# A linear-attention and Hadamard feed-forward block: weight sums moved within attention, stores issued later, staged tokens read earlier, down weights split in two stages

## Chip, cores and metric

The kernel runs on one core of one Trainium2 chip. The metric is the device time of one execution in microseconds (us), given as the median of several executions. The profile is of one further execution.

## The reference, cut to what matters

4096 tokens of width 512, all in float32. Attention is causal linear attention with 16 query heads and 4 key/value heads of width 128; a feed-forward block with Walsh-Hadamard transforms (fwht) follows. Both have a residual and a layer norm without weights.

```
q, k, v = x @ Wq.T, x @ Wk.T, x @ Wv.T        # 16, 4, 4 heads of 128
q, k = rope(q), rope(k);  qf, kf = elu(q) + 1, elu(k) + 1
for each token s:                             # running sums over the tokens
    state += kf[s] outer v[s];  z += kf[s]
    out[s] = (qf[s] @ state) / (qf[s] @ z + 1e-6)
x = layernorm(x + out @ Wo.T)
y = fwht(x * SU_ug) / 64
up, gate = y @ W_up.T * (Ws_up * 64), y @ W_gate.T * (Ws_gate * 64)      # 2048 each
h = fwht(silu(gate) * up * SU_dp) / 64
x = layernorm(x + h @ W_down.T * (Ws_dp * 64))
```

## The kernel before

**Number form.** Each operand of a large product is split into a high part, a rounded copy made by ScalarE, and a low part, the difference, made by VectorE or GpSimd (`hilo`, L88 to L90). A product is three matmuls: high by high, high by low, low by high.

**Order.** All DMAs are issued from SyncE's queue by the helper `dma`, whose call is L58, so all of them have that one line. The program is written as Python loops with generators that are stepped by hand (`step`, `go`). The order on each engine is then decided by the tile framework's planner (`TileContext(..., schedule_with_timeline_sim=True)`), which goes through its own simulated time: program order is a priority, and an instruction whose inputs and buffers are there can go ahead of it. Each engine, SyncE's queue too, then runs its own list strictly in order, and a waiting instruction holds all behind it. A pool has a fixed number of buffers for each tag.

**Stages.** There are four:

1. *Attention* (L127 to L507). 16 blocks of 256 tokens are gone through twice, once for each half of the heads: n = 0 to 31, with four slots in each n for its two key heads and two pairs of 64-token chunks. The weights of one half take 24 of the 28 buffers of the pool `wres` (tag `w`, 2 KB each in a partition). In the first half, `load_x` loads and splits the tokens and stores the parts to `xs_d`; the second half loads those parts. `wcomb(p)` prepares gate and up weights for a later stage: it loads four quarter matrices of `wug` into four `wres` buffers, forms four sums and differences on GpSimd (L394) and stores them to `was_d`. It is called in n = 3 to 10.
2. *Wo stage* (L600 to L755). 32 tiles of 128 tokens. For each, numerators are multiplied by the reciprocal of the denominators (`norm_o`), 48 matmuls form the output projection (`ps_wo`, L722), x is added (L734) and, for each two tiles, `layer_norm` normalises the pair, which is stored to `y_d`. From each of the first 12 pairs `wo_front` makes the transformed tokens for gate and up: transpose, sign, Hadamard matmul, butterflies, and seven combinations (`YKEY`) stored to `yq_d` by `put`. `prep_down` transforms the down weights and stores their seven combinations to `wdop_d`. The tile loop steps each front three times for each tile (`fr`). Transformed tokens of the first quarter are loaded by `yload` into the pool `yop` (16 buffers of 4 KB) and split by `ysplit` from tile 26 on.
3. *Gate and up* (L758 to L890). 32 stages: four quarters f of 1024 tokens by eight pairs p of weight tiles. Each stage has seven products s = 0 to 6 (`SEQ`: a seven-multiplication scheme of Strassen's kind for 2 by 2 blocks), each for gate and for up with six matmuls of 128x512 (L833). Results are combined and passed through SiLU; gate times up on GpSimd (L816) gives the blocks H, of which four more combinations are formed on GpSimd (`hS`, L887). Seven blocks a stage go to `hop_d`. `asplit(n + 1, s)` and `aload(n + 2, s)` prepare the next stages' weights. Fronts of the last four pairs run inside stages 1, 3, 5 and 7, with temporaries in the tag `x4` (`xtile`, 2 buffers), which the token loads of later quarters use too. In the last stage (n = 31), `split_b(s)` splits all seven sets of down weights.
4. *Down* (L893 to L985). 8 units of 512 tokens, each with seven products of 48 matmuls of 128x256 (L951). `h_load` fetches four raw tiles for each product, `h_split` splits them, the residual from `y_d` is added, and `finish` normalises and stores the output.

Raw weights of gate and up are loaded into tag `ar` (10 buffers) of the pool `g1`, which closes with stage 3; raw operands of down into tag `hr` (8 buffers) of the pool `d1`, which opens with stage 4 on the same memory.

Of the kernel before, what the change touches and what calls it, by code (L numbers as in the profile page):

```python
# [43 lines left out]
def kernel(  # L44
# [95 lines left out]
    with ExitStack() as es:  # L140
# [296 lines left out]
        for i, (n, g, p) in enumerate(slots):  # L437
# [62 lines left out]
            if sl == (1, 0) and 3 <= n < 11:  # L500
                wcomb(n - 3)
# [41 lines left out]
    def front(i, y2, spool, ptr, phd, alloc):  # L543
        f, c = divmod(i, 4)
        d = alloc[1]([128, 2, 4, 128], F32, "fd")
        for e in range(2):
            ps = ptr([128, 4, 128], "ps_tr")
            for k in range(4):
                T.transpose(ps[:, k], y2[e][:, k * 128:(k + 1) * 128], idt)
            for k in range(4):  # L550
                S.activation(ps[:, k], ps[:, k], AF.Copy, scale=sut[:, k:k + 1])
            hl = alloc[0]([128, 2, 4, 128], F32R, "fhl")
            hilo(hl[:, 0], hl[:, 1], ps)
            yield
# [12 lines left out]
        G.tensor_tensor(q[:, 1], d[:, :, 0:2], d[:, :, 2:4], ALU.subtract)  # L567

        def put(key, x):
            dma(yq_d[f][YKEY.index(key)][:, :, c * 128:(c + 1) * 128], x)  # L570

        put("B11", q[:, 0, 0])
        put("B21", q[:, 1, 0])
        put("B22", q[:, 1, 1])
        put("T3", d[:, 1, 2:4])
        yield
        tt = alloc[1]([128, 3, 2, 128], F32, "ft")
        G.tensor_tensor(tt[:, 0], q[:, 0, 1], q[:, 0, 0], ALU.subtract)
# [43 lines left out]
    with ExitStack() as es:  # L622
# [89 lines left out]
        for t in range(32):  # L712
# [23 lines left out]
            if t % 2:  # L736
                layer_norm(p2, [yp[:, 0], yp[:, 1]], "r1")
                for j in range(2):
                    dma(y_d[t - 1 + j], yp[:, j])
                if t < 24:  # L740
                    fr.append(wo_front(t // 2, [yp[:, 0], yp[:, 1]]))
            if t >= 1:
                step(gd, 4)
            for x in list(fr):
                step(x, 3)
            fr = fr[-2:]
            if 26 <= t:
                for s in ((t - 26,) if t < 31 else (5, 6)):
                    YOPS[s] = ysplit(s, yload(0, s))
# [8 lines left out]
    pgu = ctx.enter_context(tc.tile_pool(name="pgu", bufs=2, space=PSUM, reuse_waits="tile"))  # L758
    BW = [None] * 7

    with ExitStack() as es:
# [5 lines left out]
        def araw(name):  # L767
            return pa.tile([128, 2, 2, 128], F32, tag="ar", name=name, bufs=10)
# [11 lines left out]
        def load_b(s):  # L780
            RAW["b", s] = []
            for j in range(4):
                x = pa.tile([128, 2, 256], F32, tag="ar", name="braw", bufs=10)
                dma(x, wdop_d[s][:, 2 * j:2 * j + 2])
                RAW["b", s].append(x)

        def split_b(s):
            raw = RAW.pop(("b", s))
            ops = [[], []]
            for j in range(2):  # L790
                hl = [wres.tile([128, 2, 256], F32R, tag="w", name=x) for x in ("wdh", "wdl")]
                hilo(*hl, raw[j])
                for l in range(2):
                    ops[l] += [hl[l][:, 0], hl[l][:, 1]]
            hl = [ytile([128, 4, 256], F32R, x) for x in ("wdzh", "wdzl")]
            for j in range(2):
                hilo(hl[0][:, 2 * j:2 * j + 2], hl[1][:, 2 * j:2 * j + 2], raw[2 + j], G if j else V)
            for l in range(2):
                ops[l] += [hl[l][:, r] for r in range(4)]
            BW[s] = ops  # L800

# [3 lines left out]
        yraw = []  # L805
        fr = None
        for n in range(NS):
# [11 lines left out]
            if n in (1, 3, 5, 7):  # L819
                fr = ff_front(12 + n // 2)  # L820
            new = {}
            for s, tag in enumerate(SEQ):
# [3 lines left out]
                for u in (1, 0):  # L826
# [20 lines left out]
                    if s == 5:  # L847
# [30 lines left out]
            def put(key):  # L878
# [3 lines left out]
            for key in ("A11", "A12", "A22"):  # L882
                put(key)
            for key, x0, x1, op in (("S1", "A21", "A22", ALU.add), ("S3", "A11", "A21", ALU.subtract),
# [3 lines left out]
                put(key)  # L888


    with ExitStack() as es:
        pd = es.enter_context(tc.tile_pool(name="d1", bufs=2, reuse_waits="tile"))
        units = [(f, jp) for f in range(4) for jp in range(2)]  # L893
# [4 lines left out]
        HR, HOP, YN, bank = {}, {}, {}, {}  # L898

        def h_load(n, s):  # L900
            f, jp = units[n]
            HR[n, s] = []
            for qd in range(4):
                raw = pd.tile([128, 2, 256], F32, tag="hr", name="hraw", bufs=8)
                dma(raw, hop_d[f][s, jp, :, 2 * qd:2 * qd + 2])
                HR[n, s].append(raw)
            if s == 0:
                YN[n] = []
                for half in range(2):
                    y = (pd.tile([128, 2, 512], F32, tag="yn", name="yres") if half else  # L910
                         xtile([128, 2, 512], F32, "yres"))
                    for j in range(2):
                        dma(y[:, j], y_d[8 * f + 2 * (2 * jp + j) + half])
                    YN[n].append(y)

        def h_split(n, s):
            HOP[n, s] = []
            for qd, raw in enumerate(HR.pop((n, s))):
                hi, lo = (pd.tile([128, 2, 256], F32R, tag="ad", name=x, bufs=20) for x in ("hah", "hal"))
# [11 lines left out]
        h_load(*order[0])  # L931
        h_load(*order[1])
        h_split(*order[0])
        for idx, (n, s) in enumerate(order):
            if idx + 2 < len(order):
                h_load(*order[idx + 2])
            if idx + 1 < len(order):
                h_split(*order[idx + 1])
# [91 lines left out]
```

## Time and profile before

| what | before |
|---|---|
| median of 3 runs (lowest to highest) | 2380.95 us (2379.08 to 2382.65) |
| the profiled execution: its time, its span | 2373.57 us, 2371.9 us |
| mean granted TensorE clock | 0.988 |
| busy: TensorE, VectorE, ScalarE, GpSimd | 2272.3, 1818.6, 1402.0, 1246.1 us |
| DMA traffic, mean rate | 484.16 MB, 204 GB/s |

PE is TensorE, DVE VectorE, ACT ScalarE, POOL GpSimd, and SPq SyncE's queue, which issues the DMAs. Rows name an instruction by its line and by output<-inputs. A busy share is an average over four stages with different limits, so it is to be read by stage: attention lies at about 0 to 970 us, the Wo stage at 970 to 1368, gate and up at 1368 to 2024, and down at 2041 to 2372. The chain of waits is the work that ended last, followed back from the end.

### The profile page before, as it was taken

To read this page: it belongs to the slowest core of one execution; us is meant where nothing else is said; L and a number is where in the kernel's file an instruction comes from. 1 tells how busy PE (TensorE), PEld (TensorE's weight loads), DVE (VectorE), ACT (ScalarE), POOL (GpSimd) and SP (SyncE) were. 2 spreads that over 40 slices of the span, in tenths; PEclk is the share of its full clock that TensorE was granted. 3 is DMA by queue.
4 is the path that set the end of the run, shared out by engine and by line. 5 is a ranking of instruction groups with operands and counts; after the bars stand their busy time and mean duration, and the time that the engine had idled before them with its cause. 6 is when DMAs were issued, how large, how long until landed. Compare 5 with 4: busy or idle time off the path is not lost.

```text
span 2371.9 us, 42234 instructions
## 1 busy us (share of the span) xinstructions
PE 2272.3 (96%) x14432; PEld 2014.1 (85%) x14432; DVE 1818.6 (77%) x2799; ACT 1402.0 (59%) x2482; POOL 1246.1 (53%) x1000
## 2 busy tenths in 40 slices
PE   7999999999999998999999999999999999699998
PEld 6888999989999998788887778778878887699998
DVE  7999998998888889678887776666766767565554
ACT  5666777777777777444443466555655656455553
POOL 3676454454444445377878435555565556533332
PEclk9999999999999999999999999999999999899999
DMA  7676555554444545979897876776765766777673
GB/s 237 212 226 183 168 150 149 157 155 130 132 134 135 141 143 138 304 241 293 272 282 232 283 235 202 243 230 188 225 211 189 240 189 205 235 227 250 222 254 125
DMA packets 369528, 484.16 MB, mean 204 GB/s; under 512 B 68670, under 2 KB 224384, under 8 KB 365344
## 3 DMA queue, kind: packets, MB, share of 16 engines
q1 hardware_dynamic: 369312, 481.45, 65.7%
q8 instruction: 114, 1.87, 0.3%
q14 instruction: 102, 0.84, 0.1%
HBM read 282.76 MB, written 156.76 MB: 185 GB/s over the span
## 4 chain that ended last, share of the span: by engine, by line
PE 78%; DVE 11%; DMA 4%; issue 3%; ACT 3%; POOL 1%; SPq 0%; DVEq 0%; ACTq 0%; POOLq 0%
PE ps_wo L722 15%; PE ps_a L833 13%; PE ps_qk L244 11%; PE ps_da L951 8%; PE ps_b L833 7%; PE ps_num L371 4%; PE ps_db L951 4%; PE ps_c L833 4%; PE ps_s L294 3%; PE ps_v L197 2%; PE ps_dc L951 2%; DVE x L230 1%; DVE sw L234 1%; DVE ps_qk L227 1%; PE ps_sc L337 1%
## 5 line engine op out<-in xcount | busy, mean ns | idle before, releaser
L351 POOL TENSOR_SCALAR_AFFINE_SELECT A<-A 64x512 fp32r<-64x512 f32 x256 | 222.2, 868 | 294.9 <-DVE am L347 197.1
L244 PE MATMUL ps_qk<-xh,wh 128*128 128x256 f32 x1280 | 360.3, 281 | 11.5 <-DVE x L230 7.0
L244 PE MATMUL ps_qk<-xl,wh 128*128 128x256 f32 x1280 | 358.0, 280 | 2.4 <-DVE xl L90 2.4
L244 PE MATMUL ps_qk<-xh,wl 128*128 128x256 f32 x1280 | 357.9, 280 | 0.2 <-DVE wl L90 0.2
L90 DVE TENSOR_TENSOR wol<-A,woh 128x512 fp32r<-128x512 f32 x217 | 228.5, 1059 | 110.9 <-ACT woh L89 91.2
L816 POOL TENSOR_TENSOR cc<-cc 128x512 f32<-128x512 f32 x96 | 146.9, 1532 | 300.7 <-ACT cc L813 153.0
L226 POOL TENSOR_TENSOR sw<-sw,csb 128x512 f32<-128x512 f32 x160 | 220.4, 1379 | 146.1 <-ACT sw L225 136.7
L244 PEld LDWEIGHTS ps_qk<-xh,wh 128*128 128x128 f32 x1280 | 243.3, 190 | 14.0 <-ACT qh L323 3.1
L244 PEld LDWEIGHTS ps_qk<-xl,wh 128*128 128x128 f32 x1280 | 242.6, 190 | 3.7 <-DVE xl L90 2.7
L244 PEld LDWEIGHTS ps_qk<-xh,wl 128*128 128x128 f32 x1280 | 242.6, 190 | 1.5 <-DVE wl L90 0.4
L89 ACT ACTIVATE hah<-hraw 128x512 fp32r<-128x512 f32 x224 | 140.7, 631 | 153.0 <-PE ps_da L951 74.3
L89 ACT ACTIVATE woh<-A 128x512 fp32r<-128x512 f32 x217 | 135.7, 630 | 134.8 <-PE ps_b L833 71.7
L90 POOL TENSOR_TENSOR hal<-hraw,hah 128x512 fp32r<-128x512 f32 x80 | 105.6, 1323 | 207.0 <-ACT hah L89 173.0
L833 PE MATMUL ps_a<-yoh,woh 128*128 128x512 f32 x512 | 202.8, 397 | 3.8 <-ACT sv L840 3.8
L833 PE MATMUL ps_a<-yol,woh 128*128 128x512 f32 x512 | 202.5, 395 | 0.0
L833 PE MATMUL ps_a<-yoh,wol 128*128 128x512 f32 x512 | 199.1, 396 | 0.0
L90 DVE TENSOR_TENSOR hal<-hraw,hah 128x512 fp32r<-128x512 f32 x144 | 103.7, 726 | 123.2 <-ACT hah L89 110.8
L722 PE MATMUL ps_wo<-wh,oh 128*128 128x512 f32 x448 | 179.1, 400 | 11.0 <-DVE yp L734 8.2
L722 PE MATMUL ps_wo<-wh,ol 128*128 128x512 f32 x448 | 178.5, 399 | 0.0
L722 PE MATMUL ps_wo<-wl,oh 128*128 128x512 f32 x448 | 178.2, 398 | 0.0
L840 ACT ACTIVATE sv<-ps_a,wsc 128x512 f32<-128x512 f32 x192 | 127.0, 679 | 43.0 <-PE ps_a L833 42.9
L231 ACT ACTIVATE sw<-x,neg 128x512 f32<-128x512 f32 x160 | 115.3, 721 | 54.5 <-DVE x L230 52.4
(215 smaller groups left out, 7283.1 us busy)
## 6 DMA issues: line engine op xcount, KB each, us to landing
hraw<-hop_d SPq DMA_DIRECT2D x224, 256.0 KB
vd<-vhl SPq DMA_DIRECT2D x128, 256.0 KB
num_d<-num SPq DMA_DIRECT2D x128, 256.0 KB
rb<-rec_d SPq DMA_DIRECT2D x128, 256.0 KB
hop_d<-hS SPq DMA_DIRECT2D x128, 256.0 KB
nt<-num_d SPq DMA_DIRECT2D x31, 1024.0 KB
A<-in_wug_dram SPq DMA_DIRECT2D x93, 256.0 KB
hop_d<-cc SPq DMA_DIRECT2D x64, 256.0 KB
```

The lines of the kernel that those rows point to most:

```text
L89: S.activation(hi, src, AF.Copy)
L90: eng.tensor_tensor(lo, src, hi.bitcast(F32), ALU.subtract)
L226: G.tensor_tensor(sw, sw, sinb, ALU.mult)
L231: S.activation(sw, x1, AF.Exp, bias=neg1)
L244: T.matmul(ps[:, j], W[key][wa][:, k * 128:(k + 1) * 128], B[xa][:, k], start=i == 0, stop=i == 11)
L351: G.affine_select(ah, ah.bitcast(F32), pattern=[[0, 8], [1, 64]], compare_op=ALU.is_ge, fill=0.0, base=0, channel_multiplier=-1)
L371: T.matmul(ps[:, c2], l, r, start=i == 0, stop=i == len(ops) - 1)
L722: T.matmul(ps, l[:, h], r, start=i == 0, stop=i == 47)
L816: G.tensor_tensor(x, x, c.pop(("g", q)), ALU.mult)
L833: T.matmul(ps, w[:, u, k], y[:, k], start=first and i == 0, stop=i == 5, skip_group_check=not first)
L840: S.activation(x, ps, AF.Copy, scale=sc)
L951: T.matmul(ps[:, j], ops[qd][al][:, r, js], BW[s][bl][ip], start=first and i == 0, stop=i >= 45, skip_group_check=True)
```

## The change

- `wcomb` is called in n = 18 to 25, in the second half of attention, instead of n = 3 to 10.
- `front` has two more pauses, one ahead of each group of `put` calls; up to three fronts instead of two are kept in the list.
- A pair of normalised tiles is stored to `y_d` one tile later (the last pair at once).
- Token loads and splits of the first quarter are called at tiles 24 to 30 instead of 26 to 31. Those of a later quarter are called two ahead, the first two of them at the end of stage p = 6.
- Fronts in gate and up start in stages 1, 2, 4, 5; an unfinished one is first stepped to its end.
- The stores of a stage's seven blocks to `hop_d` are called in the next stage, after s = 1, 2, 3, three at a time; the last stage's follow the loop.
- A pool `rp` of 10 raw buffers outlives both stages: it holds raw gate and up weights, raw down weights and raw down operands. In stage n = 31 only three sets of down weights are split, and the first operand of down is loaded; the other four sets are split in the first four steps of the first down unit. The residual's load is called at s = 3 of the unit before. The operand splits of down have 19 buffers instead of 20.

```diff
-            if sl == (1, 0) and 3 <= n < 11:
-                wcomb(n - 3)
+            if sl == (1, 0) and 18 <= n < 26:
+                wcomb(n - 18)
...
+        yield
         put("B11", q[:, 0, 0])
...
+        yield
         put("T1", tt[:, 0])
...
                 layer_norm(p2, [yp[:, 0], yp[:, 1]], "r1")
-                for j in range(2):
-                    dma(y_d[t - 1 + j], yp[:, j])
+                ylast = yp
...
+            if t % 2 == 0 and t or t == 31:
+                for j in range(2):
+                    dma(y_d[t - t % 2 - 2 * (t < 31) + j], ylast[:, j])
...
-            fr = fr[-2:]
-            if 26 <= t:
-                for s in ((t - 26,) if t < 31 else (5, 6)):
-                    YOPS[s] = ysplit(s, yload(0, s))
+            fr = fr[-3:]
+            if 24 <= t < 31:
+                YOPS[t - 24] = ysplit(t - 24, yload(0, t - 24))
...
+    rp = ctx.enter_context(tc.tile_pool(name="rp", bufs=10, reuse_waits="tile"))
...
-            if n in (1, 3, 5, 7):
-                fr = ff_front(12 + n // 2)
+            if n in (1, 2, 4, 5):
+                step(fr, 9)
+                fr = ff_front(12 + (1, 2, 4, 5).index(n))
...
+                if n and s in (1, 2, 3):
+                    for _ in range(3):
+                        if late_puts:
+                            late_puts.pop(0)()
...
-                        if s == 0:
-                            yraw = [yload(f + 1, 0)]
-                        if s < 6:
-                            yraw.append(yload(f + 1, s + 1))
                         new[s] = ysplit(s, yraw[s])
+                        if s < 5:
+                            yraw.append(yload(f + 1, s + 2))
                     else:
                         if s == 0:
                             load_b(0)
                             load_b(1)
-                        split_b(s)
-                        if s + 2 < 7:
-                            load_b(s + 2)
+                        if s in (1, 3, 5):
+                            split_b(s // 2)
+                        if s == 1:
+                            load_b(2)
+                        if s == 5:
+                            h_load(0, 0)
                 step(fr)
+            if p == 6 and f < 3:
+                yraw = [yload(f + 1, 0), yload(f + 1, 1)]
...
-            for key in ("A11", "A12", "A22"):
-                put(key)
+            late_puts = [lambda k=k, put=put: put(k) for k in ("A11", "A12", "A22", "S1", "S3", "S2", "S4")]
...
-                put(key)
+        for put in late_puts:
+            put()
...
-        h_load(*order[0])
+        h_split(*order[0])
         h_load(*order[1])
-        h_split(*order[0])
+        load_b(3)
+        y_load(0)
         for idx, (n, s) in enumerate(order):
-            if idx + 2 < len(order):
-                h_load(*order[idx + 2])
             if idx + 1 < len(order):
                 h_split(*order[idx + 1])
+            if n == 0 and s + 3 < 7:
+                split_b(s + 3)
+            if idx + 2 < len(order):
+                h_load(*order[idx + 2])
+            if n == 0 and s + 4 < 7:
+                load_b(s + 4)
+            if s == 3 and n + 1 < len(units):
+                y_load(n + 1)
```

More of the change, by code (lines that the diff above doesn't have):

```diff
@@ L758, with h_load, load_b, split_b @@
     pgu = ctx.enter_context(tc.tile_pool(name="pgu", bufs=2, space=PSUM, reuse_waits="tile"))
+    rp = ctx.enter_context(tc.tile_pool(name="rp", bufs=10, reuse_waits="tile"))
     BW = [None] * 7
+    HR, HOP, YN, bank = {}, {}, {}, {}
+    units = [(f, jp) for f in range(4) for jp in range(2)]
+    def h_load(n, s):
+        f, jp = units[n]
+        HR[n, s] = []
+        for qd in range(4):
+            raw = rp.tile([128, 2, 256], F32, tag="ar", name="hraw")
+            dma(raw, hop_d[f][s, jp, :, 2 * qd:2 * qd + 2])
+            HR[n, s].append(raw)
+    def load_b(s):
+        RAW["b", s] = []
+        for j in range(4):
+            x = rp.tile([128, 2, 256], F32, tag="ar", name="braw")
+            dma(x, wdop_d[s][:, 2 * j:2 * j + 2])
+            RAW["b", s].append(x)
+    def split_b(s):
+        raw = RAW.pop(("b", s))
+        ops = [[], []]
+        for j in range(2):
+            hl = [wres.tile([128, 2, 256], F32R, tag="w", name=x) for x in ("wdh", "wdl")]
+            hilo(*hl, raw[j])
+            for l in range(2):
+                ops[l] += [hl[l][:, 0], hl[l][:, 1]]
+        hl = [ytile([128, 4, 256], F32R, x) for x in ("wdzh", "wdzl")]
+        for j in range(2):
+            hilo(hl[0][:, 2 * j:2 * j + 2], hl[1][:, 2 * j:2 * j + 2], raw[2 + j], G if j else V)
+        for l in range(2):
+            ops[l] += [hl[l][:, r] for r in range(4)]
+        BW[s] = ops
     with ExitStack() as es:
@@ L767, in araw @@
         def araw(name):
-            return pa.tile([128, 2, 2, 128], F32, tag="ar", name=name, bufs=10)
+            return rp.tile([128, 2, 2, 128], F32, tag="ar", name=name)
         def ff_front(i):
@@ L778, in ff_front @@
                              lambda s, n: pgu.tile(s, F32, tag="a", name=n, bufs=4), (ytile, xtile))
[L780 to L800, printed above, removed]
         for s in range(7):
@@ L804 @@
         NS = 32
-        yraw = []
+        yraw, late_puts = [], []
         fr = None
@@ L870, with put @@
                             load_b(1)
-                        split_b(s)
-                        if s + 2 < 7:
-                            load_b(s + 2)
+                        if s in (1, 3, 5):
[4 more added lines that the diff above has]
+                            h_load(0, 0)
                 step(fr)
+            if p == 6 and f < 3:
+                yraw = [yload(f + 1, 0), yload(f + 1, 1)]
             YOPS.update(new)
             H = {"A11": c["h", 0], "A12": c["h", 2], "A21": c["h", 1], "A22": c["h", 3]}
-            def put(key):
+            def put(key, f=f, p=p, H=H):
                 dma(hop_d[f][WKEY.index(key)].rearrange("j p i t -> p j i t")[:, :, p],
                     H[key].rearrange("p (j t) -> p j t", j=2))
-            for key in ("A11", "A12", "A22"):
-                put(key)
+            late_puts = [lambda k=k, put=put: put(k) for k in ("A11", "A12", "A22", "S1", "S3", "S2", "S4")]
             for key, x0, x1, op in (("S1", "A21", "A22", ALU.add), ("S3", "A11", "A21", ALU.subtract),
@@ L887 @@
                 G.tensor_tensor(H[key], H[x0], H[x1], op)
-                put(key)
+        for put in late_puts:
+            put()
     with ExitStack() as es:
         pd = es.enter_context(tc.tile_pool(name="d1", bufs=2, reuse_waits="tile"))
-        units = [(f, jp) for f in range(4) for jp in range(2)]
         order = [(n, s) for n in range(len(units)) for s in range(7)]
@@ L897, with y_load @@
             order.insert(order.index((n - 1, 5)), (n, 0))
-        HR, HOP, YN, bank = {}, {}, {}, {}
-        def h_load(n, s):
+        def y_load(n):
             f, jp = units[n]
[L902 to L914, printed above, removed]
+            YN[n] = []
+            for half in range(2):
+                y = (pd.tile([128, 2, 512], F32, tag="yn", name="yres") if half else
+                     xtile([128, 2, 512], F32, "yres"))
+                for j in range(2):
+                    dma(y[:, j], y_d[8 * f + 2 * (2 * jp + j) + half])
+                YN[n].append(y)
         def h_split(n, s):
@@ L918, in h_split @@
             for qd, raw in enumerate(HR.pop((n, s))):
-                hi, lo = (pd.tile([128, 2, 256], F32R, tag="ad", name=x, bufs=20) for x in ("hah", "hal"))
+                hi, lo = (pd.tile([128, 2, 256], F32R, tag="ad", name=x, bufs=19) for x in ("hah", "hal"))
                 hilo(hi, lo, raw, G if qd == 1 or (qd == 3 and s % 2) else V)
@@ L929, in finish @@
                 dma(out[t * 128:(t + 1) * 128], y[:, j])
-        h_load(*order[0])
+        h_split(*order[0])
         h_load(*order[1])
-        h_split(*order[0])
+        load_b(3)
+        y_load(0)
         for idx, (n, s) in enumerate(order):
+            if idx + 1 < len(order):
+                h_split(*order[idx + 1])
+            if n == 0 and s + 3 < 7:
+                split_b(s + 3)
             if idx + 2 < len(order):
                 h_load(*order[idx + 2])
-            if idx + 1 < len(order):
-                h_split(*order[idx + 1])
+            if n == 0 and s + 4 < 7:
+                load_b(s + 4)
+            if s == 3 and n + 1 < len(units):
+                y_load(n + 1)
             tag = SEQ[s]
```

## The prediction

> **What bounds the kernel now.** I read the page first, then the busy time of each stage, then the waits of TensorE and the chain of waits at the places where a stage loses time.
>
> ```profile
> PE 2272.3 (96%) x14432; PEld 2014.1 (85%) x14432; DVE 1818.6 (77%) x2799; ACT 1402.0 (59%) x2482; POOL 1246.1 (53%) x1000
> ```
>
> TensorE is busy for 96% of the span: no edit that only unloads another engine gains anything by itself. What can be had is the roughly 100 us in which TensorE idles, or runs thinner than elsewhere. Where that is, the stages show (us, busy time of each engine with instructions in brackets, granted clock, DMA share, GB/s):
>
> ```profile
> 60.00:240.00 180.00, 165.61 (x1283) 153.76 (x1282) 172.24 (x249) 120.39 (x218) 121.25 (x100) 0.98 0.69 210
> 240.00:400.00 160.00, 160.00 (x1312) 152.74 (x1310) 147.89 (x248) 121.81 (x220) 80.75 (x75) 1.00 0.51 147
> 600.00:760.00 160.00, 159.64 (x1297) 151.78 (x1296) 138.94 (x238) 117.56 (x208) 76.65 (x77) 1.00 0.50 139
> 1360.00:1420.00 60.00, 54.79 (x237) 43.09 (x235) 45.54 (x64) 39.67 (x68) 18.42 (x13) 1.00 0.74 245
> 1520.00:1580.00 60.00, 53.19 (x221) 41.27 (x221) 43.62 (x52) 38.13 (x66) 31.70 (x22) 0.97 0.80 255
> 1580.00:1680.00 100.00, 100.00 (x430) 80.53 (x429) 63.77 (x72) 51.79 (x87) 56.78 (x39) 1.00 0.62 194
> 2000.00:2060.00 60.00, 39.82 (x232) 34.30 (x231) 41.96 (x42) 29.75 (x51) 38.11 (x25) 0.86 0.71 234
> 2060.00:2340.00 280.00, 280.00 (x2358) 280.00 (x2357) 161.94 (x330) 145.69 (x240) 90.69 (x70) 1.00 0.72 234
> ```
>
> From 60 to 240 VectorE is full (172.2 of 180) and TensorE waits for it; once that is over, TensorE never pauses. The stages 1580:1680 and 2060:2340 are free of stalls. Holes are at 1360 to 1420, 1520 to 1580, and 2000 to 2060. The same view of the projections alone (L244) gives the first loss exactly: 685 matmuls in 180 us, then 686 in 160, so **20 us** go there.
>
> ```profile
> 60.00:240.00 180.00, 91.43 (x685) 85.22 (x686) 0.98 0.69 210
> 240.00:400.00 160.00, 87.63 (x686) 82.19 (x684) 1.00 0.51 147
> ```
>
> What differs between the two windows is the weight sums (the rows of tile wq: duration min/median/max in ns, first and last start):
>
> ```profile
> L58 SPq DMA_DIRECT2D wq<-in_wug_dram x32: 539/580/1059, 31.5 to 191.8; - x32
> L394 POOL TENSOR_TENSOR wq<-wq x32: 1262/1299/1782, 37.4 to 204.5; 128x512 f32<-128x512 f32 x32
> ```
>
> They stand in the program at blocks 3 to 10 of 28 us each (the chain repeats its projections at 637.41 and 665.35), but were issued from 31.5: the planner pulls work ahead as soon as its buffers are free. Two stalls of the issuing queue (start, duration, instruction), and after them the chain of waits at the last boundary:
>
> ```profile
> 1355.97 2.48 SPq L58 DMA_DIRECT2D yraw<-yq_d  x5
> 1374.18 1.03 SPq L58 DMA_DIRECT2D y_d<-yp  x2
> 1375.32 0.39 SPq L58 DMA_DIRECT2D yraw<-yq_d  x1
> ```
>
> ```profile
> 2022.35 1.44 PE ps_b L833 x5
> ...
> 2033.25 1.27 POOL hS L887
> ...
> 2034.53 0.36 SPq L58
> ...
> 2034.99 5.02 DMA hraw<-hop_d
> ...
> 2040.77 7.62 PE ps_da L951 x48
> ```
>
> SP stands from 1358 to 1374 at the store of the last normalised tile, with one token load and all loads of the next stage's weights behind it. At 2023.8 TensorE finishes gate/up; it starts on down at 2040.8, because the first load of down's operand stood behind four stores that waited for GpSimd.
>
> **The change part by part.** Sums are against the profiled execution (2373.57, span 2371.9); the median is 7.4 us (0.3%) above it, and I take the saving off the median.
>
> *Weight sums moved from blocks 3-10 to 18-25.* Each block moves 4 loads, 4 sums on POOL, 4 stores. They can't slide back to the start if the planner hands out a pool's buffers in program order: now they come behind the second half's weights, whose last load is at 479 in the chain. That order shows in this trace: token loads for quarter 1 are issued at 1514 only, though their two buffers and data were there from about 1370. So they run from about 480 on. Gone at the start: of the 20 us I take 17 back (the initial weight splits remain; ends 10 and 20), and 2 before 60, where two blocks' 4 MB share the DMA with weights on the chain (0 to 4).
> What they cost in the second half: VectorE needed 172.2 against 147.9 us for the same projections, so 24.3 us more for the 27 sums between 60 and 240, 0.90 each (ql went from 879 to 1004 ns, sw from 680 to 952). 32 sums add 28.8 us. They take 8 x 23.9 us (37.4 to 204.5 is seven steps), 191 us, and VectorE idles 21.1 of 160 at 600:760, so 25.2 in 191. The deficit is 3.6, but idle time behind ScalarE isn't all usable: I take **8** (ends 2 and 20).
> Here a rule speaks against the change. The Trainium skill, page "SBUF — State Buffer", section "Who interferes with whom", says that a VectorE operation with two SBUF inputs and a GpSimd operation that reads SBUF exclude each other for a whole instruction. The trace agrees in kind (the split wdl takes 677 ns at best and 1786 at worst). By the rule every sum could block VectorE for its whole 1.30 us: 41.6 us, a deficit of 16, and attention would gain 3. By the row it gains 17 + 2 - 8 = **11**. I take the row, since it is measured on these instructions; the rule's figure goes into the range.
>
> *Wo stage (front's puts one or two steps later, y_d a tile later, token loads two tiles earlier).* TensorE waits once, 8.2 us (ps_wo for DVE yp, a late load of x_n at 1298.6 behind the transposes of an older pair). A pair's yp buffer now comes free one tile (11.3 us) later; one tile of margin is left. The front's buffers are held longer by the same shift. Gain 8 if the stall falls away, loss 4 if a second one comes: **2**.
>
> *Start of gate/up.* The seven yraw loads are now all in the program before the last y_d store. TensorE idles 5.2 us at 1360:1420, partly for yraw, partly for A splits (chain, 1400.96, 2.82) that stay behind y_d as before. **3** (0 to 5).
>
> *Quarter changes.* Two token tiles are read a stage ahead, and the fronts run in stages 1, 2, 4, 5 and leave the shared x4 buffers before stage 7, where now the fourth front and the token loads want the same two. Lost at 1520:1580: 6.8 idle, and 1.8 at the lower clock (0.97 of 60). **7** of 8.6 (low end 3). Later quarter changes lose almost nothing.
>
> *hop_d stores a stage later.* 7 DMAs a stage are issued after s = 1, 2, 3 of the next one, behind fewer waits (SP waits 107.5 us for hS in all). Stages without stalls are already full, so **0**. The cover is buffer slack: the tile of A11 is wanted 16 allocations on, at s = 6 of the next stage, some 17 us in, while its store leaves about 6 us in.
>
> *Boundary to down.* 232 matmuls at 2000:2060 are about 86 at 0.233 and 146 at 0.119 us, 37.4 us: **22.5** lost. 3.7 of it is the last gate/up stage itself, in which 7 splits of down weights (28 pairs of hi and lo) crowd VectorE; 17 the gap; 1.9 the slow first group (7.62 against 5.71). Now 3 splits stay, and the first operand is loaded before the stores. What comes instead: 1 us in the last stage; 4 at the gap (hah 0.63, hal 0.7 to 1.78, then hal on POOL, which may queue behind cc and four hS, 7 us); and four steps of the first unit with a split each. Such a step has 8 ScalarE copies of 0.631 (5.05 us, of 5.71 that TensorE needs), 5 or 6 VectorE splits (0.69 to 1.78: 4 to 10 us), 8 loads of 256 KB (2.1 MB, 6.1 us at the 345 GB/s reached at 2040:2060), and a ring of 10 raw buffers that lets only one step run ahead. I take 6.7 us a step, so 4 lost (1 to 15). Gain 22.5 - 9 = **13.5** (3 to 19). The other steps keep their cost; one operand buffer fewer (19) is covered, as 8 belong to a step.
>
> Sum: 11 + 2 + 3 + 7 + 0 + 13.5 = 36.5, so 2380.95 - 36.5 = **2344**. All low ends together leave about 0, all high ends about 60.
>
> **The rivals.** *Given back (2367).* VectorE fills up in the second half (attention gains 0) and the first unit takes 9 us a step (another 11 lost): 36.5 - 22 = 14.5. For: the rule above and 17.4 of 20 us busy already. Against: POOL is a third emptier there.
> *The sums don't move (2355).* The planner gives them the four free weight buffers at 31 us again: 25.5 remain. For: they ran 100 us ahead before. Against: the order of token loads.
> *Slower (2421).* The late stores hold the 16 u buffers, and the cc at s = 6 waits in each of 31 stages; at 2.5 us each that is 77 us against 36.5. From 1.3 us a stage on, the change loses. For: a store stuck in SP's queue delays all behind it (15.7 us once). Against: 10 us of slack by the count above.
>
> **How the numbers follow.** Forecast 0.66 (its own range 2328 to 2360), given back 0.16, sums in place 0.08, late stores 0.06, and 0.04 that most parts reach their high ends (2322). I leave out the late stores and some of both tails: 2322 to 2368. About 0.2% (4.8 us) is what measuring can tell from no change; only given back reaches into it, with 0.04, and 0.02 beyond. Faster 0.88, same 0.04, slower 0.08.
>
> **What would show it.** Right: tile wq starts after 480; 60:240 holds over 720 projection matmuls; VectorE over 95% at 480:670; no yraw wait near 1549; the gap before the first ps_da under 6 us, and its first four groups 6 to 7.5 us each. Wrong: wq near 31; TensorE waiting for DVE at 500 to 650; ps_b or cc waiting for hop_d stores in each stage.

## The result, and the profile after

| | before | after |
|---|---|---|
| median (lowest to highest), 4 runs each | 2381.8 us (2379.08 to 2383.36) | 2347.04 us (2345.34 to 2349.16) |
| ratio to before, 95% interval | | 0.9856 (0.9839 to 0.9873) |
| the profiled execution: its time, its span | 2373.57, 2371.9 us | 2347.88, 2345.7 us |

The change saves 34.8 us by the medians. Between the two profiled executions it is only 26.2 us, because the profiled execution of before was a good one, about 8 us under its kernel's median. A second profile of the same kernel (experiment e1) has a span of 2380.1 us. So both stand in the table below, which splits the span at instructions of TensorE that are the same in both kernels:

| stretch of TensorE's work | before | before again (e1) | after | saved, by the one and the other | predicted |
|---|---|---|---|---|---|
| attention: start to the last projection | 934.7 | 937.5 | 937.1 | -2.4 / 0.4 | 11 |
| Wo stage: from there to the last `ps_wo` | 432.7 | 435.1 | 427.1 | 5.6 / 8.0 | 2 |
| the first 168 matmuls of gate and up | 43.4 | 43.4 | 41.7 | 1.7 / 1.7 | 3 |
| the 169th to the 1344th (first quarter change) | 294.5 | 296.7 | 283.4 | 11.1 / 13.3 | 7 |
| the 1345th to the 2604th | 294.7 | 294.7 | 294.8 | -0.1 / -0.1 | 0 |
| from there to the end (boundary to down) | 371.9 | 372.7 | 361.6 | 10.3 / 11.1 | 13.5 |
| sum | 2371.9 | 2380.1 | 2345.7 | 26.2 / 34.4 | 36.5 |

Attention, where the prediction looked for 11 us, gained nothing. The saving came from the later stages, and two of them gave more than was forecast.

The totals of the page hardly show it; TensorE has the same work in a shorter span:

```profile
PE 2270.4 (97%) x14432; PEld 2014.8 (86%) x14432; DVE 1808.5 (77%) x2799; ACT 1403.3 (60%) x2482; POOL 1244.4 (53%) x1000
```

The busy time of each stage in the profile after (window, length, then busy time and instructions of PE, PEld, DVE, ACT and POOL, granted clock, DMA share, GB/s) shows where the holes were filled and where a new one is:

```profile
60.00:240.00 180.00, 180.00 (x1464) 171.60 (x1463) 168.77 (x280) 136.71 (x247) 88.56 (x82) 0.99 0.52 148
240.00:400.00 160.00, 159.90 (x1307) 152.54 (x1307) 146.86 (x242) 121.58 (x218) 80.55 (x75) 1.00 0.53 155
480.00:660.00 180.00, 164.66 (x1263) 154.07 (x1264) 150.33 (x233) 112.06 (x201) 121.99 (x107) 0.97 0.66 200
1360.00:1420.00 60.00, 59.25 (x255) 46.34 (x254) 45.51 (x69) 40.67 (x73) 20.46 (x15) 1.00 0.68 226
1520.00:1580.00 60.00, 60.00 (x259) 48.32 (x258) 48.83 (x52) 37.95 (x61) 36.90 (x23) 1.00 0.82 258
2000.00:2060.00 60.00, 50.30 (x385) 48.41 (x386) 41.47 (x50) 33.95 (x57) 35.18 (x25) 0.94 0.87 283
```

60:240 is now full, 1464 matmuls instead of 1283. 1360:1420 and 1520:1580 have lost their stalls, and 2000:2060 holds 385 matmuls instead of 232. But 480:660, which had no loss worth naming before, is now short: 164.66 us and 1263 matmuls. The same view of the projections alone (L244; before: 685 and 756 in these two windows):

```profile
60.00:240.00 180.00, 98.54 (x768) 92.58 (x768) 0.99 0.52 148
480.00:660.00 180.00, 86.58 (x647) 81.40 (x648) 0.97 0.66 200
```

83 projections more in the first window, 109 fewer in the second. The loss moved with the sums. Where these stand now, the rows of tile wq say (duration min/median/max in ns, first and last start in us):

```profile
L58 SPq DMA_DIRECT2D wq<-in_wug_dram x32: 539/577/782, 459.4 to 622.0; - x32
L394 POOL TENSOR_TENSOR wq<-wq x32: 1260/1291/1749, 477.8 to 630.2; 128x512 f32<-128x512 f32 x32
```

They moved as forecast, with the first loads 20 us before the 480 named there, and one sum still takes 1.29 us (the median). The waits of after in 480:680 (engine, line and tile that waited, releaser, total us, times, longest) show what they do there:

```profile
ACT sw L231 <- DVE x L230: 47.3, 29, 4.5
DVE x L230 <- POOL sw L226: 22.4, 10, 5.6
...
POOL wq L394 <- DMA wq<-in_wug_dram: 15.2, 7, 5.0
...
PE ps_num L371 <- POOL A L351: 10.5, 9, 3.2
...
PE ps_sc L337 <- DVE A L348: 6.1, 5, 2.2
```

GpSimd stands 15.2 us at sums whose loads have not landed. Behind them in its queue are `sw` (L226) and the masks `A` (L351). VectorE idles 22.4 us for `sw`, and TensorE waits for `A` of GpSimd and of VectorE. So VectorE is not full in 480:660 (150.33 of 180). But the queue is only one part: VectorE's instructions are also longer there, 645 ns on the mean (150.33 us for 233) against 578 without any sums (e4: 158.40 us for 274), which is some 15 us. Experiment e5 takes the two apart as far as they can be.

The issuing queue at the end of the Wo stage (start, duration, instruction) answers the stall shown before. It still stands until 1371.6 at the last `y_d` stores, but the token loads are now ahead of them, and only the next weights behind:

```profile
1354.33 1.02 SPq L58 DMA_DIRECT2D y_d<-yp  x2
1355.40 0.97 SPq L58 DMA_DIRECT2D yraw<-yq_d  x2
1371.60 1.03 SPq L58 DMA_DIRECT2D y_d<-yp  x2
1372.73 1.27 SPq L58 DMA_DIRECT2D A<-in_wug_dram  x2
```

At the boundary to down the gap is gone: TensorE's last gate/up matmul ends at 2005.0 and its first of down at 2005.7. But then it stands. Its waits between 1990 and 2060 (before: one of 16.8 us):

```profile
PE ps_da L971 <- DVE hal L90: 5.7, 1, 5.7
PE ps_da L971 <- DVE yres L978: 2.7, 2, 1.6
PE ps_a L848 <- ACT sv L855: 0.9, 1, 0.9
PE ps_da L971 <- ACT hah L89: 0.7, 1, 0.7
```

VectorE's rows in order of time name what the `hal` itself waited for (in brackets the idle time before it):

```profile
2005.09 0.75 DVE L860 SCALAR_TENSOR_TENSOR cc<-ps_b,wsc,sv 128x512 f32<-128x512 f32 x1 [0.64 <-PE ps_b L848]
2011.18 0.69 DVE L90 TENSOR_TENSOR hal<-hraw,hah 128x512 fp32r<-128x512 f32 x1 [5.34 <-POOL hS L908]
```

`hal` reads nothing that the last stage's `hS` on GpSimd makes. Yet this `hal` and two starts of ScalarE's `hah` (2009.83 and 2013.03) each come within 0.04 us of the end of an `hS` (2011.15, 2009.80, 2012.99). Their pool opens on the memory of the pool that closes with stage 3; e7 below tests whether it is that memory that they wait for. The first four groups of 48 matmuls took 13.2, 7.5, 5.8 and 7.0 us, and 5.7 from then on.

### The profile page after: what moved, and what is told of

It is laid out like the page before. It is cut to its first block, busy times and chain, and to the rows that moved or that the text cites. A ratio compares the mean times of both kernels' runs of the same rounds, so it can differ in the third digit from the quotient of the medians.

```text
span 2345.7 us, 42356 instructions
## 1 busy us (share of the span) xinstructions
PE 2270.4 (97%) x14432; PEld 2014.8 (86%) x14432; DVE 1808.5 (77%) x2799; ACT 1403.3 (60%) x2482; POOL 1244.4 (53%) x1000
## 4 chain that ended last, share of the span: by engine, by line
PE 78%; DVE 8%; DMA 6%; issue 4%; POOL 2%; ACT 2%; SPq 1%; DVEq 0%; ACTq 0%; POOLq 0%
PE ps_a L848 14%; PE ps_qk L244 13%; PE ps_wo L724 12%; PE ps_da L971 8%; PE ps_b L848 7%; PE ps_num L371 5%; PE ps_db L971 4%; PE ps_c L848 3%; PE ps_s L294 3%; PE ps_v L197 3%; PE ps_dc L971 2%; PE ps_sc L337 1%; PE ps_den L372 1%; PE ps_sc L338 1%; SPq L58 1%
## 5 line engine op out<-in xcount | busy, mean ns | idle before, releaser
L351 POOL TENSOR_SCALAR_AFFINE_SELECT A<-A 64x512 fp32r<-64x512 f32 x256 | 219.1, 856 | 289.5 <-DVE am L347 185.7
L244 PE MATMUL ps_qk<-xh,wh 128*128 128x256 f32 x1280 | 359.8, 281 | 7.6 <-ACT wh L89 3.9
L244 PE MATMUL ps_qk<-xh,wl 128*128 128x256 f32 x1280 | 358.1, 280 | 0.0
L244 PE MATMUL ps_qk<-xl,wh 128*128 128x256 f32 x1280 | 358.0, 280 | 0.0
L226 POOL TENSOR_TENSOR sw<-sw,csb 128x512 f32<-128x512 f32 x160 | 219.9, 1375 | 143.3 <-ACT sw L225 135.2
L244 PEld LDWEIGHTS ps_qk<-xh,wh 128*128 128x128 f32 x1280 | 243.5, 190 | 9.2 <-ACT wh L89 4.1
L244 PEld LDWEIGHTS ps_qk<-xl,wh 128*128 128x128 f32 x1280 | 242.9, 190 | 1.3
L244 PEld LDWEIGHTS ps_qk<-xh,wl 128*128 128x128 f32 x1280 | 242.9, 190 | 0.8
L90 DVE TENSOR_TENSOR hal<-hraw,hah 128x512 fp32r<-128x512 f32 x144 | 106.2, 746 | 117.0 <-PE ps_da L971 41.8
```

What stands on the lines that cost most here:

```text
L90: eng.tensor_tensor(lo, src, hi.bitcast(F32), ALU.subtract)
L226: G.tensor_tensor(sw, sw, sinb, ALU.mult)
L244: T.matmul(ps[:, j], W[key][wa][:, k * 128:(k + 1) * 128], B[xa][:, k], start=i == 0, stop=i == 11)
L351: G.affine_select(ah, ah.bitcast(F32), pattern=[[0, 8], [1, 64]], compare_op=ALU.is_ge, fill=0.0, base=0, channel_multiplier=-1)
```

## The experiments

**e1, before once more.** No edit.

> The kernel before itself, once more, with its own profile. The profiled execution of before took 2373.57 us where its timed executions lie at 2379 to 2383, so about 8 us of the 34.8 us gained are in no trace. If that execution was only a good one, this profile shows a span near 2378 to 2381 and the extra microseconds spread or in one place of attention; if profiling itself makes before faster, it is near 2372 again. Ratio 1.000 within 0.002.

Ratio 1.0 (0.9992 to 1.0009), 2378.59 us. Against the first profile its span is 8.2 us longer, in steps of at most 3 us: 2.8 in attention, 2.4 in the Wo stage, 2.2 in the first quarter of gate and up, 0.8 at the end. Differences of up to about 3 us between single profiles of two kernels, in one stretch, are thus not evidence of anything.

**e2, the move of the sums alone, and e3, everything but it.**

```diff
e2, in before:
-            if sl == (1, 0) and 3 <= n < 11:
-                wcomb(n - 3)
+            if sl == (1, 0) and 18 <= n < 26:
+                wcomb(n - 18)
e3, in after: the same two lines the other way round
```

> Before with one edit: the weight sums called in blocks 18 to 25. By the prediction's sum attention gains 11 us: 2371, ratio 0.9954. By the two traces (TensorE's half of attention 24.5 us earlier, its end 2.5 us later) the second half gives all of it back: 2384, ratio 1.001, with the projections of 60:240 at over 750 matmuls and those of 480:660 at about 650.

> The changed kernel with the weight sums back in blocks 3 to 10. By the prediction it loses 11 us against the changed kernel: 2358, ratio 0.990. By the traces it loses nothing or gains 2 us: 2345, ratio 0.9847, with 60:240 at about 686 projection matmuls again and 480:660 full.

e2: 1.0001 (0.9992 to 1.0009). e3: 0.9854 (0.984 to 0.9869), against 0.9856 of after. By both ways the move is worth nothing. The trace of e2 shows that it is not that nothing happens: half of the projections are done 25.4 us earlier than in before (460.1 instead of 485.5), the last 0.2 us earlier (934.5 instead of 934.7). Against e1's profile of before these are 28.3 and 3.0 us; the second half costs 25 us by both. What the first half gains, the second gives back. It gained more than the 19 us forecast; the price in the second half was 25 where 8 was taken.

**e4, no sums at all.** Their loads, sums and stores are left out, and the stages of gate and up that would read the sums read unsummed quarters of the weights.

```diff
-            if sl == (1, 0) and 18 <= n < 26:
-                wcomb(n - 18)
...
-            dma(x, was_d[p][key].rearrange("p (u k m) -> p u k m", u=2, k=2))
+            dma(x, wug[2 * p + (key in ("S1", "S2"))].rearrange("p (u k m) -> p u k m", u=2, k=4)[:, :, 0:2])
```

> The changed kernel without the weight sums: their 32 loads, sums and stores are left out, and gate and up take unsummed quarters of the same size in their place. If the sums cost what the gap in the second half shows (about 27 us), this takes 2320, ratio 0.974. If the prediction's 8 us for the second half were right after all and something else slowed the second half, it takes 2339, ratio 0.982.

0.9757 (0.9742 to 0.9772). Attention ends at 906.1 us: 28.6 earlier than in before, 31.0 earlier than in after. So the 32 sums cost 29 us at the start and 31 in the second half, 0.9 to 1.0 us each. Both windows of the projections hold some 770:

```profile
60.00:240.00 180.00, 100.47 (x781) 94.34 (x782) 1.00 0.53 152
480.00:660.00 180.00, 100.26 (x768) 93.42 (x768) 1.00 0.48 135
```

**e5, after with loads a block ahead and the sums pinned.** One sum in each slot of blocks 18 to 25, held behind GpSimd's instruction before it in the program, so that the planner cannot pull it ahead.

```diff
-                G.tensor_tensor(r[o], r[a], r[b], op)
+            tc.keep_in_program_order(G.tensor_tensor(r[o], r[a], r[b], op))
...
-            if sl == (1, 0) and 18 <= n < 26:
-                wcomb(n - 18)
+            if sl == (1, 1) and 17 <= n < 25:
+                wload(n - 17)
+            if 18 <= n < 26:
+                wsum(n - 18, i % 4)
```

> The changed kernel with the sums of block n called one in each of its four slots and held behind GpSimd's instructions before them in the program, and their loads called a block earlier. The same 32 sums meet VectorE in the same half, but GpSimd should not stand at a load. If the 27 us of the second half come from GpSimd waiting for the loads (15.2 us seen) with the rope product behind it, 15 to 20 us come back: about 2328, ratio 0.978. If they come from the two engines excluding each other, it stays where the changed kernel is: ratio 0.9856, within 0.002.

0.9835 (0.982 to 0.985): between the two cases expected. No row of a sum waiting for its loads is left, and attention ends 8.8 us earlier than in after (928.3; in e7 to e10, which have after's code for attention, it ends at 934.2 to 937.3). That is the part of the queue and of the pace together, since the 32 sums now start over 236 us instead of 152. Of the 22.4 us that VectorE idled for `sw`, 15.1 are still there (440:940), so not all of them came from waiting loads. And attention still ends 22 us behind e4. The sums now run from 573.2 to 810, and there TensorE is short of work while VectorE is over 90% busy (e5):

```profile
660.00:820.00 160.00, 150.64 (x1181) 139.22 (x1180) 147.66 (x225) 107.90 (x191) 105.41 (x89) 1.00 0.63 188
```

Against after in the same window (140.42 for 241 instructions) VectorE does fewer instructions in more time: 656 ns on the mean instead of 583. VectorE's rows by shape say which of them grew. First after, which has no sums in this window, then e5 (behind the count: us in all, mean ns of one):

```profile
L312 DVE TENSOR_TENSOR sl<-s,sh 128x512 fp32r<-128x512 f32 x12 | 8.2, 679 | 0.0
...
L227 DVE TENSOR_TENSOR ps_qk<-ps_qk,csb 128x512 f32<-128x512 f32 x29 | 20.1, 693 | 9.1 <-ACT sw L225 9.0
```
```profile
L312 DVE TENSOR_TENSOR sl<-s,sh 128x512 fp32r<-128x512 f32 x10 | 16.5, 1651 | 0.0
...
L227 DVE TENSOR_TENSOR ps_qk<-ps_qk,csb 128x512 f32<-128x512 f32 x26 | 18.0, 691 | 3.4 <-ACT sw L225 3.0
```

`sl` has both inputs in SBUF, and it takes over twice as long in e5; so does `kft` (678 and 1781 ns). `ps_qk` has one input in PSUM, and it did not grow at all. That is what the rule of the Trainium skill that the prediction cites describes (page "SBUF — State Buffer", section "Who interferes with whom"). Over all shapes the growth is about 20 us for the 20 sums of this window, 1.0 us a sum (an estimate: growth of each mean times the count). That is the price which e4 measured.

**e6, the sums spread evenly.** As e5, but one sum in every third slot from block 0 to 23, over both halves.

```diff
+            if i == 0:
+                wload(0)
+            if i % 3 == 2 and i < 96:
+                wsum(i // 12, i // 3 % 4)
+                if i // 3 % 4 == 3 and i < 95:
+                    wload(i // 12 + 1)
```

> The changed kernel with the 32 sums held in place one in each third slot, from block 0 to block 23, their loads called right after the last sum of the four before. If waiting behind loads and bunching is the cost, nearly all of it goes: 2322 to 2328, ratio 0.976 to 0.979. If a sum costs its 0.9 us of VectorE wherever it stands, and TensorE waits for that in the first half as it did before, about half remains: ratio 0.981. If neither, 0.9856.

0.9804 (0.979 to 0.9819), 2330.33 us: the fastest complete version of this study, with the interval apart from that of after. Attention ends at 923.1, 17.0 us behind e4: 0.53 a sum. About 12 us are lost by the time that half of the projections are done (469.9 us, e4 458.0), with 18 sums behind it: 0.66 each. The same 32 instructions cost 31 us in a lump, 22 when pinned in blocks 18 to 25 (e5), and 17 in a thin row. They did not become cheaper for VectorE: over 60:460 its instructions grow by about 18 us against e4 (an estimate as in e5) for the 18 sums, 1.0 us each as before. What changed is how much of that TensorE had to wait for.

**e11, the sums of e6 on VectorE, and e12, only those of the first half there.**

```diff
-            tc.keep_in_program_order(G.tensor_tensor(r[o], r[a], r[b], op))
+            tc.keep_in_program_order(V.tensor_tensor(r[o], r[a], r[b], op))
e12: V for the first 21 sums, G for the other 11
```

> As e6 (one sum in every third slot, blocks 0 to 23, pinned; ratio 0.9804), with the 32 sums on VectorE instead of GpSimd. If what a sum costs is that GpSimd's read of two SBUF operands keeps VectorE's two-input operations out (1.30 us at each sum), 0.69 us of VectorE's own time is cheaper: attention ends 5 us or more earlier than e6's, ratio 0.978. If it is VectorE's time that counts, whoever takes it (0.5 us a sum net in e6), 0.69 us of a VectorE that is 94% busy costs the same or more: 0.980 to 0.983. If it is the loads and stores of the sums (8 MB in all), nothing changes: 0.9804.

> As e6 (one sum in every third slot, blocks 0 to 23, pinned), with the 21 sums of the first half of attention on VectorE, where e11 lost nothing against e4 (half of the projections at 456.5 us, e4 458.0, e6 469.9), and the other 11 on GpSimd, where e6 lost about 5 us and e11 some 23 (VectorE stood 28 us for reloaded denominators). If the two halves add up: attention ends near 911 us, ratio 0.975 to 0.978. If the second half's loss follows from the order that the planner finds and not from the engine of the sums, it can come back: 0.980 to 0.987.

e11: 0.9869 (0.9848 to 0.989). e12: 0.9827 (0.9811 to 0.9843). Each is slower than e6, though each is ahead of it by the middle of attention. Half of the projections are done at 456.5 us in both, against 458.0 in e4 and 469.9 in e6: in the first half a sum on VectorE, 0.69 us of an engine that is 97% busy, costs nothing that can be seen, where the same sum on GpSimd costs 0.66. Loads and stores are the same in all three, so they are not the price of a sum there. From the middle to the last projection e11 takes 21 us more than e6, and e12 23; e11 loses another 8 us between the last projection and the first `ps_wo` (41.3 us, e6 33.2). In the second half VectorE stands at reloaded denominators, which only that half has. Its waits there in 480:820, of e11, e12 and e6, one row each:

```profile
DVE dn L111 <- DMA dn<-den_d: 28.1, 9, 4.6
```
```profile
DVE dn L111 <- DMA dn<-den_d: 18.6, 6, 5.2
```
```profile
DVE dn L111 <- DMA dn<-den_d: 4.0, 3, 2.8
```

In e12 the second half's program is nearly that of e6, its sums on GpSimd but for the first three, and the wait is there all the same. So it does not come from the engine of these sums; that the planner's order makes it is the likely cause, but is not shown. Nor does the wait by itself account for what is lost: it is 14.6 us longer than e6's in e12 and 24.1 in e11, where these halves are 23 and 21 us longer. In kind it is the wait of `wq` once more: an instruction that stands in its engine's list ahead of its load's landing, and holds everything behind it.

**e8, the quarter changes as before.**

```diff
-            if n in (1, 2, 4, 5):
+            if n in (1, 3, 5, 7):
...
-            if p == 6 and f < 3:
-                yraw = [yload(f + 1, 0), yload(f + 1, 1)]
(and the loads of stage 7 one product ahead instead of two)
```

> The changed kernel with the quarter changes as before: fronts in stages 1, 3, 5, 7 and token loads one product ahead instead of two, called from s = 0 on. By the prediction (7 us for this part) and by the traces (8.2 us between stages 8 and 16, the first quarter change among them) it loses 7 to 9 us: ratio 0.989. If the late hop_d stores and not the token loads cleared SP's queue there, it loses under 2 us.

0.9933 (0.9916 to 0.995). The 169th to the 1344th matmul take 294.7 us, as in before (294.5), and 283.4 in after: the 11.3 us are this part's. The fronts' stages and the loads' order were put back together, so the share of each is open. The window of e8, and its chain of waits there (start, us, what):

```profile
1520.00:1580.00 60.00, 53.56 (x213) 41.90 (x213) 39.17 (x47) 32.89 (x57) 33.37 (x24) 0.91 0.74 231
```
```profile
1546.58 1.24 DVE yol L596
...
1547.84 6.10 DMA yraw<-yq_d
...
1556.89 3.63 DMA yraw<-yq_d
```

With one load ahead, a token load goes only when the split of an earlier tile is done (the one at 1547.84 follows `yol`, L596), and two of them, 6.10 and 3.63 us, stand on the chain. Another 4.3 us went at the boundary to down (365.9 instead of 361.6), where nothing was edited; which order of the planner did that was not followed up.

**e10, the Wo stage as before.** Fronts without their two pauses and two in the list, `y_d` stored with its own pair, token loads from tile 26.

```diff
-        yield
         put("B11", q[:, 0, 0])
...
-                ylast = yp
+                for j in range(2):
+                    dma(y_d[t - 1 + j], yp[:, j])
...
-            fr = fr[-3:]
+            fr = fr[-2:]
```

> As after, but the Wo stage as before: puts of the front without the two pauses, two fronts in the list, y_d stored with its own pair, token loads of the first quarter at tiles 26 to 31. By the two traces (Wo stage 5.6 us shorter, the start of gate/up 0.8 longer) it loses 4 to 6 us against after: 2352, ratio 0.988. By the sum of the prediction (2 in the Wo stage, 3 at the start of gate/up) 5 us as well, but with more than half of them after the last ps_wo. Rival: the wait of 8 us for yp was chance of the order that the planner found: ratio stays 0.9856.

0.9899 (0.9884 to 0.9913). The Wo stage takes 436.7 us instead of 427.1, and TensorE's old stall is back (e10; before: 8.2):

```profile
PE ps_wo L722 <- DVE yp L734: 8.6, 1, 8.6
```

So it was not chance: these edits took it away. The stall stands in all four profiles without them (before, e1, e2, e10: 8.1 to 8.6 us) and in none of the other ten. They were undone together, so which of the three did it is open. The first 168 matmuls of gate and up take 41.8 us in e10 too, so the 1.7 us saved there do not need the early token loads, against the prediction's step. They may be no saving at all: e7 and e8, with the early loads, take 43.4 and 42.8, and before 43.4.

**e9, all seven sets of down weights split in the last gate/up stage.** The first operand is still loaded ahead of the last stores.

```diff
-                        if s in (1, 3, 5):
-                            split_b(s // 2)
+                        split_b(s)
...
-            if n == 0 and s + 3 < 7:
-                split_b(s + 3)
```

> As after, but all seven sets of down weights are split in the last gate/up stage (n = 31), as in before; the first operand of down is still loaded ahead of the last stores. My theory of the prediction: the crowded last stage costs some 4 us again, GpSimd still has four hal and the splits ahead of the first operand's, and the first unit gets back what it loses now (11 us in its first four groups, of which the first group's wait of 5.7 us for one hal is not the splits' doing): the stretch from the last products to the 240th matmul of down changes by -5 to +3, so 2342 to 2351, ratio 0.984 to 0.988. Rival: the early operand alone made the gain and the four moved splits only cost: 6 to 8 us better than after, ratio 0.982. Second rival: the splits fill the ring of 10 raw buffers, the first operand comes late again, and 10 us or more go: 0.990.

0.988 (0.9865 to 0.9895). From the 2604th matmul to the end it takes 367.7 us: 4.2 less than before, 6.1 more than after. Of the boundary's 10.3 us the early operand alone thus gives 4.2, and the splits' delay 6.1. The last stage (to 2006 us) with VectorE at 20.23 of 22 us in e9, and at 13.68 in after:

```profile
1984.00:2006.00 22.00, 20.24 (x85) 15.44 (x83) 20.23 (x18) 15.85 (x29) 16.83 (x11) 1.00 0.72 218
```
```profile
1984.00:2006.00 22.00, 20.40 (x87) 15.84 (x86) 13.68 (x16) 10.68 (x18) 13.97 (x11) 1.00 0.64 192
```

The crowding costs e9 3.1 us up to the last gate/up matmul, 3.4 in the gap, and 2.7 in the first group; its next four groups take 22.9 us instead of 26.0. So four splits in the first unit cost 3.1 us, where the prediction took 4, and give 9.2. The 3.1 is a rough figure: in the other profiles with the same splits these four groups take 23.6 to 28.1 us, so 0.7 to 5.2 more than e9's.

**e7, the ring of u buffers shifted by eight.** The blocks of gate and up lie in 16 buffers (tag `u`) that are used in turn; eight more tiles at the start move each block to another one. If the first group's wait of 5.7 us is one for memory, that should move it.

```diff
         yraw, late_puts = [], []
+        for _ in range(8):
+            V.memset(utile("pad")[:, 0:1], 0.0)
```

> The changed kernel with eight more one-element tiles taken from the ring of u buffers at the start of gate and up, which shifts which buffer each block of the last stage gets. At the start of down ScalarE's hah waits 4.2 and 2.6 us for GpSimd's hS, though it reads nothing of it. If it waits for the buffers (the operand pool lies on the memory of the ring, whose last tiles hS still reads), the shift frees them, the first group of ps_da takes 7 us where it took 13.2, and 4 to 6 us are gained: ratio 0.983. If the order of the queues makes it wait, nothing changes: 0.9856.

0.9883 (0.9864 to 0.9903), with a median of 2347.79 us and a span of 2346.5, against 2345.7 of after: no gain. But the wait changed its place and its releaser, in ScalarE's rows of e7:

```profile
2008.55 1.15 ACT L89 ACTIVATE hah<-hraw 128x512 fp32r<-128x512 f32 x2 [2.17 <-POOL cc L832]
2015.10 4.27 ACT L89 ACTIVATE hah<-hraw 128x512 fp32r<-128x512 f32 x8 [5.40 <-DMA hop_d<-hS]
```

`hah` reads `hraw` alone. That it waits for another tile's user, a store of `hS`, when only the addresses of the u tiles were changed shows, as far as the profile names the releaser rightly, that the memory is what it waits for. The gain expected did not come: the shift put another late tile there, so what the group would take without this wait is not measured.

## Why the prediction was right, and where it was not

The forecast of 2344 us was 3 us off, the sum of 36.5 close to 34.8. But it was close because errors of about 10 us on either side met, and only the experiments show that.

- **Attention, 11 predicted, nothing measured.** The step that failed is "I take 8 (ends 2 and 20)" for the second half. It is 25 us in e2 and 27 in after, past its upper end. The gain at the start was put at 19 and came out at 25. The working set 25 us of VectorE's idle time, as seen at 600:760, against the sums' 28.8 us. In after nothing of it was usable: the 32 sums cost 31 us (e4), near the 28.8 with nothing taken off. Two things go into that. First, the pace: the prediction spread the sums over 191 us, but they started over 152 (in before over 167, by the very row that it quotes), which leaves 20 us of such idle time and not 25. Second, GpSimd's queue, in which the sums waited 15.2 us for their loads with `sw` behind them. The row for it stood in the profile of before, in the waits of 60:240, and the prediction passed it by:

```profile
POOL wq L394 <- DMA wq<-in_wug_dram: 14.2, 5, 3.9
```

  In e5 both together are worth 8.8 us of the 31. The other 22 are what TensorE feels of the 1.0 us by which each sum lengthens VectorE's work (the rows of e5).
- **The rule against the row.** The Trainium skill, page "SBUF — State Buffer", section "Who interferes with whom", made the gain 3; the row made it 11; it was -2.4 and 0.4 by the two profiles. The rule came nearer, and the prediction chose the row. But the rule's sum was near by luck: its 1.30 us a sum is too much, and the same idle time was set against it. The row, 0.90 us a sum at the start, was right as a price (e4: 0.9 there, 0.97 in after); the mistake was to set idle time against it. The rule has the kind right: by e5's rows the operations with two inputs in SBUF pay. It fits e11 too: on VectorE itself a sum of 0.69 us cost nothing in the first half, where on GpSimd it cost 0.66.
- **"Given back" half came true.** This rival had VectorE full and attention gaining nothing (it did gain nothing), and the first unit at 9 us a step (it took 13.2, 7.5, 5.8 and 7.0). Its sign, VectorE over 95% at 480:670, was also the forecast's and is wrong: 150.33 of 180 us. One of the signs of being wrong came true: TensorE waits 7.5 us for VectorE at 500 to 650.
- **Wo stage, 2 predicted, 5.6 to 8.0 measured,** 9.6 in e10. The mechanism is the one named, the stall of 8.2 us for `yp`. The term was mis-sized by hedging a gain of 8 with a loss of 4 (2 is their middle) that did not come: the longest wait of TensorE left in the stage is 4.6 us, for `oh`, and before had that one with 2.8.
- **Quarter changes, 7 predicted, 11.1 to 13.3 measured,** 11.3 in e8. The mechanism held: no wait for yraw is left at 1549. The size was taken from the losses in 1520:1580, 8.6 us; the stretch lost more than stood in that window.
- **Start of gate/up, 3 predicted, 1.7 measured,** not by the token loads, and not clear of the spread of single profiles (e10). **Late stores, 0 predicted, -0.1 measured** over 1260 matmuls in which they run in every stage. The slow rival needed 1.3 us a stage and is out.
- **Boundary, 13.5 predicted, 10.3 to 11.1 measured.** The last stage gained 3.1 us (2.7 forecast), the splits in the first unit cost about 3 (4 forecast). The step that failed is "4 at the gap": gap and first group lost 0.7 and 7.5 us over the 5.7 of a full group, 8.2 in all. The prediction saw a queue behind four `hS` as the danger for the `hal` on GpSimd; the `hal` on VectorE waited for the same `hS`, through their memory.

## What to carry to other kernels

Work that is moved to a "less busy" stretch costs there what its engine's queue and its neighbours make of it; their idle time is not simply room for it: price it at what it cost where it was, and look for a row in which the moved instruction itself waits for a load, since everything behind it waits too. Spread such work thinly and pin its place; here the same 32 sums cost 31 us bunched by the planner, 22 us pinned at one a slot, and 17 us pinned at one in every third slot. When a sum of several parts comes out right, undo the parts one by one before believing any of them.

## What the runs showed of the hardware that was not expected

- After the wait of 5.7 us in the first group of down, TensorE's matmuls of 128x256 start 0.21 us apart, not the usual 0.12, for some 2.5 us. The granted clock of after around it:

```profile
2010.00:2015.00 5.00, 3.08 (x14) 2.90 (x14) 2.00 (x2) 2.43 (x5) 4.21 (x3) 0.51 0.61 190
2015.00:2020.00 5.00, 5.00 (x44) 5.00 (x43) 5.00 (x5) 2.31 (x5) 4.70 (x3) 1.00 0.94 300
```

  The page "TensorE: Matmul & The Clock Gate" of the Trainium skill (Part 1) has this: half the clock after an idle window of about 3.4 us. Here that adds about 1.2 us to the wait (13 matmuls, 0.09 each), which is part of the 7.5 us above.
- VectorE, 97% busy in the first half of attention in e11, took 14.2 us of added sums (18 by the middle) with no loss for TensorE. A busy share of 97% was thus not a full engine. Part of such busy time is what GpSimd's instructions add to it: in e4, without any sums, `kft` takes 1126 ns on the mean in 60:240 and 681 in 480:660. That this part is what made the room is not shown.
